# Layer 0's product with its weights from seven products of blocks

## The chip, the cores and the metric

The kernel runs on one core of one Trainium2 chip. The metric is the device time of one execution in microseconds (us). Engines: PE (TensorE, matmuls; PEld its weight loads), DVE (VectorE), ACT (ScalarE), POOL (GpSimd) and SP (SyncE, which issues DMAs). Everything is 32-bit floating point; a matmul in this type leaves two records in the trace, so 16 matmuls are 32 records.

## The reference

There are 64 sequences of 32 rows of 512 values. Two layers follow each other, each with a residual connection. The change is in layer 0:

```
u = _L0_cond_ref(x, length, ...)      # masked convolution along the 512 positions, one kernel per row h, by FFT
h = relu(layernorm(u @ gw1.T + gb1) * ln_gamma + ln_beta)      # 32 values per token
gates = h @ gw2.T + gb2                                        # 8 experts
top_v, top_i = top_k(gates, 2);  top_g = softmax(top_v)
w = onehot(top_i) * top_g * (counts <= capacity)
main = u @ weight.T                                            # 2048 x 512 by 512 x 512  <- the product that is changed
lora = sum over experts of (u @ lora_A[e] * w[e]) @ lora_B[e] / 16
x = x + main + lora
```

Layer 1 (gated projections with adapters, then a mixture of 16 experts and a shared one) takes the rest of the time and is not touched.

## The kernel before

Tokens are the 64 x 32 pairs of sequence and row h, 2048 in all, in four blocks (`tb` 0 to 3) of `TB` = 512, which are eight rows h of 64 sequences. Features lie on the 128 partitions in `NC` = 4 chunks. `xT[tb]` is the residual stream of a block, 128 x 4 x 512, and `yT` the convolution's result of a block in the same form. `w0` holds the layer's weights as 128 x 4 chunks x 512 outputs, and behind them the adapters' second matrix.

PE, DVE and ACT run in the order in which the program is written (`tc.manual_schedule`); what waits at the head of an engine's queue holds all that is behind it. DMA issues of SP and POOL have their own queues. One block goes as follows:

- `convolved` (L511, L518), eight times: four matmuls by Toeplitz blocks `g`, which SP loads from `kpad` in memory, two rows h at a time; the result `y` is in one of two PSUM banks of `ps_mm`, and DVE masks it into `yT` (L518). In between stand two DVE steps of the next block's convolution kernels (`steps`, `kgen`). After the second row, `counted` (L584) adds the block before's choices up in the bank `cn`; it needs `oh`.
- `by_tokens` (L528, L535, L536), four times: `gt`, tokens by features; DVE takes the 32 gate features (`hg`), ACT the adapters' (`tmp`).
- In block 2, `gathered_down` (L466) copies adapter rows into `wr` on ACT.
- `main` (L589) for output chunk 0; `later.products` (L329, `kp`); on DVE `normed` (L543 to L559), whose square root is on ACT (L549, with a table load); `later.to_memory` (L334, L336), after which ACT writes `kpad` (L338); in block 2 `combine` (L212 to L215), in block 0 `table_rows` (L411 to L417) and zeros (`none`, L633) that POOL writes to `yd` (L636).
- `main` for chunk 1 in two halves, with `turned` (L564, `hgT`) between them; `gated` (L572, `gates`); `main` for chunk 2; on DVE `chosen` (L578, L165 to L171), twelve small dependent operations that end in `oh`; `added` (L598) for chunks 0 and 1; `main` for chunk 3; `added` for chunks 2 and 3.

The four results of `main` lie in banks of the pool `ps_acc`, which has four, one of them held by `cn` once counting has begun. Block 3 has no later block; its third and fourth part stand with the end of the layer (`weighed`, `across`, `raised`). Layer 1 already forms one of its own products from seven products of blocks (a function `seven` and the helper `TH` = 256 there); layer 0 does not.

Of the kernel before, what the change touches and what calls it, by code (L numbers as in the profile page):

```python
# [9 lines left out]
F32 = mybir.dt.float32  # L10
I32 = mybir.dt.int32
AF = mybir.ActivationFunctionType
ALU = mybir.AluOpType
# [4 lines left out]
P = 128  # L18
B, H, L = 64, 32, 512
NS = 64  # L20
TB, NTB = 512, 4
HB = TB // B
NC = L // P
# [80 lines left out]
def kernel(ctx: ExitStack, tc: tile.TileContext, a: dict, out: bass.AP):  # L104
    nc = tc.nc
    mm, tt, ts = nc.tensor.matmul, nc.vector.tensor_tensor, nc.vector.tensor_scalar
# [8 lines left out]
    ps_acc = ctx.enter_context(tc.tile_pool(name="ps_acc", bufs=4, space=PSUM))  # L115

    def bank(pool, name):
        return pool.tile([P, TB], F32, tag="bank", name=name)
# [11 lines left out]
    wl0 = first.enter_context(tc.tile_pool(name="wl0", bufs=1))  # L130
# [44 lines left out]
    xT = [xall[:, :, tb * HB : (tb + 1) * HB, :] for tb in range(NTB)]  # L175
    xT = [x.rearrange("p c h b -> p c (h b)") for x in xT]
    nc.sync.dma_start(xT[0], a["xT"][0])
    w0 = wl0.tile([P, NC + 1, L], F32, name="w0")
# [47 lines left out]
    def small(n=H):  # L226
        part = next(r for r in room if r[1] >= n)
        part[1] -= n
        return part[0][:, part[1] : part[1] + n]
# [8 lines left out]
    def run(*streams):  # L238

        while streams:  # L240
            streams = [x for x in streams if next(x, run) is not run]
# [34 lines left out]
    start = small(1)  # L276
# [70 lines left out]
    rden, t0, t1 = small(), small(), small()  # L347
# [50 lines left out]

    for _ in range(5):
        mm(bank(ps_mm, "unread"), ident, xT[0][:, 0, :], start=True, stop=True)  # L400
    second.products()
    second.to_memory()

# [46 lines left out]
    def columns(g, j):  # L450

        lo = j // NJ * RK
        src = got[g][0][:, :, lo : lo + RK, NC + j % NJ].rearrange("p (h s b) r -> p s h b r", h=2, s=2)
        for half in range(2):
            at = half * (TW + L // 2)
            to = wn[:, j, :, at : at + TW].rearrange("p s (b r) -> p s b r", r=RK)
            nc.vector.tensor_copy(to, src[:, :, half])
# [15 lines left out]
    with tc.tile_pool(name="l0", bufs=1) as l0, tc.tile_pool(name="l0b", bufs=2) as l0b:  # L473
# [45 lines left out]
            if tb in (1, 2):  # L519
                coming[0].rows(1)  # L520

        def by_tokens(tb, yT):

            for i in range(4):
                n = tb * 4 + i
                gt = bank(ps_td, f"gt_{n}")
                for c in range(NC):
                    mm(  # L528
                        gt[:, 0 : G0 + P],
                        yT[:, c, i * P : (i + 1) * P],  # L530
                        ag[:, c, :],
                        start=(c == 0),
                        stop=(c == NC - 1),
                    )
                tt(hg[:, n, :], gt[:, 0:G0], row0[:, 0:G0], ALU.add)  # L535
                nc.scalar.copy(tmp[tb][:, i, :], gt[:, G0 : G0 + P])  # L536

        def normed(tb):

            ns = slice(tb * 4, tb * 4 + 4)  # L540
            h, m, v, r, w = hg[:, ns, :], mu[:, ns], var[:, ns], rstd[:, ns], nw[:, ns]
            sq = l0b.tile([P, 4, G0], F32, tag="sq", name=f"sq_{tb}", bufs=1)
            red(m, h, AX.X, ALU.add)  # L543
            ts(m, m, 1.0 / G0, None, ALU.mult)
            tt(h, h, over(m, G0), ALU.subtract)
            tt(sq, h, h, ALU.mult)
            red(v, sq, AX.X, ALU.add)
            ts(v, v, 1.0 / G0, 1e-5, ALU.mult, ALU.add)
            nc.scalar.activation(r, v, AF.Sqrt)  # L549
            nc.vector.reciprocal(r, r)  # L550

            tt(w, r, r, ALU.mult)
            tt(w, w, v, ALU.mult)
            ts(w, w, -0.5, 1.5, ALU.mult, ALU.add)
            tt(r, r, w, ALU.mult)
            tt(h, h, over(r, G0), ALU.mult)
            tt(h, h, rows(row0[:, G0 : 2 * G0], 4), ALU.mult)
            tt(h, h, rows(row0[:, 2 * G0 : 3 * G0], 4), ALU.add)
            ts(h, h, 0.0, None, ALU.max)  # L559
# [21 lines left out]
        def counted(tb):  # L581

            for n in range(tb * 4, tb * 4 + 4):
                mm(cn[:, 0 : 2 * E0], ones, oh[:, :, n, :], start=(n == 0), stop=(n == NT - 1))  # L584

        def main(yT, ps, o, cs=range(NC)):

            for c in cs:
                mm(  # L589
                    ps,  # L590
                    w0[:, c, o * P : (o + 1) * P],
                    yT[:, c, :],
                    start=(c == 0),
                    stop=(c == NC - 1),
                )

        def added(tb, o, ps):
            tt(xT[tb][:, o, :], xT[tb][:, o, :], ps, ALU.add)  # L598

        toeplitz, coming = [], []  # L600
        for tb in range(NTB):
            if tb == 1:
                coming.append(Adapters(0))
                got = [coming[0].all()]
            yT = l0b.tile([P, NC, TB], F32, tag="yT", name=f"yT_{tb}")

            later = Kernels((tb + 1) * HB) if tb + 1 < NTB else None
            steps = later.steps() if later is not None else iter(())
            for hl in range(HB):
                convolved(tb, hl, yT)  # L610
                next(steps, None)
                next(steps, None)
                if hl == 1 and tb > 0:
                    counted(tb - 1)
                if tb == NTB - 1:
                    for j in range(hl, NF, HB):
                        columns(0, j)
            by_tokens(tb, yT)
            run(steps)
            if tb == 2:  # L620
                wr = gathered_down(0)
            ps = [bank(ps_acc, f"main_{tb}_{o}") for o in range(2)]
            main(yT, ps[0], 0)
            if later is not None:
                later.products()
            normed(tb)
            if later is not None:
                later.to_memory()
            if tb >= 2:
                combine(tb - 2)  # L630
            if tb == 0:
                table_rows()
                nc.vector.memset(none, 0.0)  # L633
                for t in range(NTU, NTE):
                    rest = yd[t * P : (t + 1) * P, :].rearrange("p (c l) -> p c l", l=P)
                    nc.gpsimd.dma_start(rest, rows(none, NC))  # L636
            main(yT, ps[1], 1, range(2))
            hT = turned(tb)
            main(yT, ps[1], 1, range(2, NC))
            gp = gated(tb, hT)  # L640
            if tb == NTB - 1:

                nc.scalar.activation(l0.tile([P, 1], F32, name="one_exp"), col(C_SGN), AF.Exp)
            ps.append(bank(ps_acc, f"main_{tb}_2"))
            main(yT, ps[2], 2)
            chosen(tb, gp)
            if tb < NTB - 1:
                added(tb, 0, ps[0])
                added(tb, 1, ps[1])
                ps.append(bank(ps_acc, f"main_{tb}_3"))  # L650
                main(yT, ps[3], 3)
                added(tb, 2, ps[2])
                added(tb, 3, ps[3])


        tt(sg[:, 1, :], best[:, 1, :], best[:, 0, :], ALU.subtract)
# [289 lines left out]
    for g in range(NG):  # L946
# [3 lines left out]
        for j in range(NF):  # L950
# [10 lines left out]
            ps = bank(ps_mm, f"gu_{g}_{j}")  # L961
# [12 lines left out]
            more = bank(ps_mm, f"gum_{g}_{j}")  # L974
# [56 lines left out]
    acc, pools, wall, places = [], [], [], []  # L1031
    routing = ExitStack()
    wide = ExitStack()

    TH = TB // 2

    def quarters(tb):

        return [xT[tb][:, k : k + 2, lo : lo + TH] for k in (0, 2) for lo in (0, TH)]

# [12 lines left out]
    def seven(tb, j, banks, si, at, done):  # L1053

        b11, b12, b21, b22 = quarters(tb)
        t1, t2, t3, t4 = diffs[tb]
        gate, up = (x.rearrange("p (k t) -> p k t", k=2) for x in (si, at))

        def products(k, *parts):
            ps = bank(banks[k % len(banks)], f"sgu_{tb}_{j}_{k}").rearrange("p (k t) -> p k t", k=2)  # L1060
            for i, (w, x) in enumerate(parts):
                w = sw[j][:, w * BW :] if w < 4 else ssw[j - 1][:, (w - 4) * BW :]
                for c in range(2):
                    mm(ps[:, i, :], w[:, c * P : (c + 1) * P], x[:, c, :], start=(c == 0), stop=(c == 1))  # L1064
            return ps

        ps = products(0, (0, b11), (6, b22))
        nc.scalar.copy(gate, ps)
        ps = products(1, (1, b21), (4, t2))
        tt(up[:, 0], gate[:, 0], ps[:, 1], ALU.add)  # L1070
        tt(gate[:, 0], gate[:, 0], ps[:, 0], ALU.add)
        tt(gate[:, 1], gate[:, 1], up[:, 0], ALU.add)
        done("gate", j)
        ps = products(2, (3, t4), (5, t3))
        tt(up[:, 1], up[:, 0], ps[:, 1], ALU.add)
        tt(up[:, 0], up[:, 1], ps[:, 0], ALU.add)
        ps = products(3, (2, t1))
        tt(gate[:, 1], gate[:, 1], ps[:, 0], ALU.add)
        tt(up[:, 1], up[:, 1], ps[:, 0], ALU.add)
# [471 lines left out]
```

## Time and profile before

| | us |
|---|---|
| median of 3 runs | 1020.14 (1019.03 to 1020.51) |
| profiled execution, its own time | 1020.05 |
| its span, first to last instruction | 1018.3 |
| PE busy in the span | 987.4 (97%) |
| DVE busy | 648.3 (64%) |
| ACT busy | 212.0 (21%) |
| block 0 of layer 0, first y to the next block's first y | 23.89 to 54.08 |
| block 1 | 54.08 to 85.07 |
| block 2 | 85.07 to 116.05 (the third's last product ends at 116.92) |
| granted TensorE clock, mean | 1.000 |

The page's row of an instruction group names line, engine, operation, output and input, count, then busy time, mean duration in ns, and the idle time of the engine just before with the work that ended it. Durations of matmuls overlap, so what one costs in a stream is read from start to start. A timeline's row has the start and the length in us, then the same names, and in brackets the idle time before it and who ended it.

### The profile page before, as it was taken

The numbers are of one execution on the slowest core, as the hardware profiler recorded it, in microseconds if no ns is written. First come the engines' busy times: TensorE is split into PE (matmuls) and PEld (weight loads), VectorE is DVE, ScalarE is ACT, GpSimd is POOL, SyncE is SP. The second block draws the span as 40 slices with busy tenths as digits, with TensorE's granted clock in tenths as the row PEclk, the third lists the DMA queues.
The fourth block names the chain that finished last, engine by engine and source line by source line (L and its number), as shares of the span: only waits on it lengthen the run. The fifth ranks groups of instructions, "written<-read, shape, count | busy, mean of one in ns | idle before, by whom it ended". The sixth has DMA issues, their size and how long they took to land. (4 is left out here: it accounts for less than half of the span.)

```text
span 1018.3 us, 16926 instructions
## 1 busy us (share of the span) xinstructions
PE 987.4 (97%) x6256; PEld 792.2 (78%) x6256; DVE 648.3 (64%) x1974; ACT 212.0 (21%) x439; POOL 170.1 (17%) x189
## 2 busy tenths in 40 slices
PE   3999999999999999999999999999999999999998
PEld 1777656888988889988889888897767677776665
DVE  6656567887666776766676767765765353333775
ACT  2322111121221311213212122121201222221100
POOL 2131001210301202102012021000000333331730
PEclk9999999999999999999999999999999999999999
DMA  6566408685665646746567557540940455555652
GB/s 187 191 224 232 136 21 301 236 294 174 224 199 192 238 164 213 248 161 214 186 198 257 175 189 238 172 141 17 409 188 1 133 167 166 166 165 199 200 176 95
DMA packets 64210, 190.62 MB, mean 187 GB/s; under 512 B 8512, under 2 KB 11616, under 8 KB 63488
## 3 DMA queue, kind: packets, MB, share of 16 engines
q1 hardware_dynamic: 49360, 138.30, 39.2%
q0 software_dynamic: 14176, 51.16, 16.2%
q8 instruction: 52, 0.85, 0.3%
q14 instruction: 30, 0.25, 0.1%
q10 hardware_dynamic: 592, 0.07, 0.1%
HBM read 158.35 MB, written 31.15 MB: 186 GB/s over the span
## 5 line engine op out<-in xcount | busy, mean ns | idle before, releaser
L885 PE MATMUL zp<-wn,at 128*128 128x288 f32 x704 | 185.4, 406 | 0.4 <-DVE at L984 0.4
L819 PE MATMUL gu<-t,w 128*128 128x128 f32 x1056 | 150.1, 278 | 0.9 <-DVE gus L966 0.9
L885 PEld LDWEIGHTS zp<-wn,at 128*128 128x128 f32 x704 | 127.1, 190 | 28.6 <-DVE at L984 0.6
L819 PEld LDWEIGHTS gu<-t,w 128*128 128x128 f32 x1056 | 135.4, 192 | 14.8 <-DVE gus L966 6.4
L444 POOL DMA_INDIRECT wa<-in_la,row_a x64 | 61.2, 956 | 299.9 <-issue 183.4
L982 ACT ACTIVATE si<-gus 128x256 f32<-128x256 f32 x88 | 36.7, 417 | 350.5 <-DVE gus L980 350.5
L819 PE MATMUL gum<-xall,w 128*128 128x128 f32 x704 | 93.0, 275 | 0.0
L819 PEld LDWEIGHTS gum<-xall,w 128*128 128x128 f32 x704 | 85.7, 192 | 0.0
L1327 PE MATMUL egu<-wall,zx 128*128 x336 | 80.6, 383 | 0.4 <-issue 0.4
L966 DVE TENSOR_TENSOR gus<-gu,los 128x512 f32<-128x512 f32 x88 | 60.6, 688 | 28.7 <-PE gu L819 26.2
L960 DVE TENSOR_TENSOR los<-los 128x512 f32<-128x512 f32 (+1 forms) x72 | 46.6, 647 | 49.9 <-ACT los L839 48.3
L1327 PEld LDWEIGHTS egu<-wall,zx 128*128 128x128 f32 x336 | 60.5, 189 | 20.0 <-ACT zx L1318 13.0
L984 DVE TENSOR_TENSOR at<-si,gus 128x256 f32<-128x256 f32 x88 | 37.4, 425 | 48.2 <-ACT si L982 48.2
L1308 POOL DMA_INDIRECT zr<-zd,tok x42 | 39.7, 946 | 159.4 <-PE zrp L1316 86.3
L839 ACT COPY los<-lo 128x512 f32<-128x512 f32 (+1 forms) x96 | 46.6, 560 | 60.1 <-PE lo L836 60.1
L1099 PE MATMUL op<-sat,sw 128*128 128x512 f32 x128 | 58.0, 595 | 0.6 <-DVE sat L1124 0.3
L589 PE MATMUL main<-yT,w 128*128 128x512 f32 x128 | 58.4, 599 | 0.0
L836 PEld LDWEIGHTS lo<-rs,wb 64*128 64x128 f32 x704 | 42.6, 187 | 16.0 <-issue 10.6
L836 PE MATMUL lo<-rs,wb 64*128 64x128 f32 x704 | 48.0, 279 | 6.1 <-DVE gus L980 5.5
L819 PE MATMUL gum<-t,w 128*128 128x128 f32 x352 | 53.7, 275 | 0.0
L819 PE MATMUL gu<-xall,w 128*128 128x128 f32 x352 | 53.7, 275 | 0.0
L1347 DVE COPY eys<-ey 128x512 f32<-128x512 f32 x42 | 29.1, 692 | 29.7 <-PE ey L1345 29.7
(316 smaller groups left out, 1452.0 us busy)
## 6 DMA issues: line engine op xcount, KB each, us to landing
w<-sums_d SPq DMA_DIRECT2D x77, 512.0 KB, 4.8
w<-in_cw SPq DMA_DIRECT2D x77, 384.0 KB, 3.4
wall<-in_xw SPq DMA_DIRECT2D x16, 768.0 KB, 15.1
yd<-eys SPq DMA_DIRECT2D x42, 256.0 KB, 2.8
g<-kpad SPq DMA_DIRECT2D x15, 512.0 KB, 5.5
w<-in_cw SPq DMA_DIRECT2D x11, 512.0 KB, 4.7
sums_d<-w SPq DMA_DIRECT2D x9, 512.0 KB, 3.6
xall<-in_xT SPq DMA_DIRECT2D x4, 1024.0 KB, 8.6
```

The lines of the kernel that those rows point to most:

```text
L444: nc.gpsimd.indirect_dma_start(to, None, src, at)
L589: mm(ps, w0[:, c, o * P : (o + 1) * P], yT[:, c, :], start=(c == 0), stop=(c == NC - 1),)
L819: mm(to, block(n, i)[:, c * P : (c + 1) * P], x[:, c], start=(c == 0), stop=(c == 1))
L836: mm(banks[which][:, at : at + P], wb[mine, lo : lo + P], r[mine, half, :], start=True, stop=True)
L839: nc.scalar.copy(to[:, first - j : first - j + n, 2 * which : 2 * which + 2], src)
L885: mm(self.zp[half][s][:, 0 : DW - TW], at[:, 1 - half, :], wn[:, j, s, lo : lo + DW - TW], start=(j == 0), stop=(j == NF - 1),)
L960: tt(lo[:, :, i], lo[:, :, i], lo[:, :, less], ALU.subtract)
L966: tt(flat, ps, adapters[:, j % 4].rearrange("p k t -> p (k t)"), ALU.add)
L984: tt(at, si, flat[:, TG:], ALU.mult)
L1099: mm(op[o], sw[j][:, i : i + P], at, start=(j == 0), stop=(j == NS1 - 1))
L1308: nc.gpsimd.indirect_dma_start(zr, None, zd[:, :], bass.IndirectOffsetOnAxis(ap=tok[:, t : t + 1], axis=0))
L1327: mm(ps[:, 0:256], x[:, c, :], wflat()[:, bass.ds(start + c * 256, 256)], start=(c == 0), stop=(c == NC - 1))
```

## The change

For blocks 0 to 2 the product of a 512 x 512 weight with a 512 x 512 block of `yT` is cut into halves of the features, of the outputs and of the tokens. Seven products of 256 x 256 x 256 blocks take the place of eight; each is four matmuls of 128 x 128 weights with 256 columns. Their operands are sums and differences: four sums of the weights (`w_sum`) are made once on DVE before the first convolution, and four differences of `yT` in every block, after each of the four tiles of `by_tokens` (the fourth is written over the part b12 of `yT`). The seven products use five banks per block: the product w12 b21 is added by PE to the bank of w11 b11 after ACT has copied that to `u`, and s4 b22 to the bank of s1 t1 after DVE has read it. DVE adds up `u` and the banks into `xT` in nine operations instead of four. `seven` is a generator; each `next(parts)` in the loop issues its next stretch, so the parts stand between the norm, `turned`, `gated` and `chosen`. After `gated` no product is left in these blocks, and the last two additions follow `chosen`. Block 3 is as before.

```diff
+    TH = TB // 2
+    w_sum = wl0.tile([P, 4, 2, TH], F32, name="w_sum")
+    w11, w12, w21, w22 = (w0[:, c : c + 2, o : o + TH] for o in (0, TH) for c in (0, 2))
+    s1, s2, s3, s4_ = (w_sum[:, i] for i in range(4))
+    tt(s1, w21, w22, ALU.add)
+    tt(s2, s1, w11, ALU.subtract)
+    tt(s3, w11, w21, ALU.subtract)
+    tt(s4_, w12, s2, ALU.subtract)
     second.products()
     second.to_memory()
...
-        def by_tokens(tb, yT):
+        def by_tokens(tb, yT, between=iter(())):
...
                 nc.scalar.copy(tmp[tb][:, i, :], gt[:, G0 : G0 + P])
+                next(between, None)
...
+        def seven(tb, yT, ps):
+            b11, b12, b21, b22 = (yT[:, c : c + 2, t : t + TH] for c in (0, 2) for t in (0, TH))
+            x11, x12, x21, x22 = (xT[tb][:, o : o + 2, t : t + TH] for o in (0, 2) for t in (0, TH))
+            diff = l0.tile([P, 3, 2, TH], F32, name=f"diff_{tb}", tag="diff")
+            t1, t2, t4 = (diff[:, i] for i in range(3))
+            t3 = b12
+            yield tt(t1, b12, b11, ALU.subtract)
+            yield tt(t2, b22, t1, ALU.subtract)
+            yield tt(t4, b21, t2, ALU.subtract)
+            yield tt(t3, b22, b12, ALU.subtract)
+            u = l0.tile([P, 2, TH], F32, name=f"u_{tb}", tag="u")
+
+            def onto(to, w, x, more=False):
+                for o in range(2):
+                    for c in range(2):
+                        nc.tensor.matmul(
+                            to[:, o],
+                            w[:, c, o * P : (o + 1) * P],
+                            x[:, c],
+                            start=(not more and o == 0 and c == 0),
+                            stop=(c == 1),
+                            skip_group_check=True,
+                        )
+
+            m1, m6 = ps(), ps()
+            onto(m1, w11, b11)
+            nc.scalar.copy(u, m1)
+            onto(m6, s2, t2)
+            yield
+            tt(u, u, m6, ALU.add)
+            tt(x12, x12, u, ALU.add)
+            onto(m1, w12, b21, True)
+            m7 = ps()
+            onto(m7, s3, t3)
+            yield
+            tt(x11, x11, m1, ALU.add)
+            tt(u, u, m7, ALU.add)
+            m5 = ps()
+            onto(m5, s1, t1)
+            tt(x21, x21, u, ALU.add)
+            tt(x22, x22, u, ALU.add)
+            yield
+            m4 = ps()
+            onto(m4, w22, t4)
+            tt(x22, x22, m5, ALU.add)
+            onto(m5, s4_, b22, True)
+            yield
+            tt(x21, x21, m4, ALU.add)
+            tt(x12, x12, m5, ALU.add)
...
-            by_tokens(tb, yT)
+            last = tb == NTB - 1
+            parts = iter(()) if last else seven(tb, yT, one)
+            by_tokens(tb, yT, parts)
             run(steps)
             if tb == 2:
                 wr = gathered_down(0)
-            ps = [bank(ps_acc, f"main_{tb}_{o}") for o in range(2)]
-            main(yT, ps[0], 0)
+            if last:
+                ps = [bank(ps_acc, f"main_{tb}_{o}") for o in range(2)]
+                main(yT, ps[0], 0)
+            next(parts, None)
             if later is not None:
                 later.products()
             normed(tb)
...
-            main(yT, ps[1], 1, range(2))
+            next(parts, None)
+            if last:
+                main(yT, ps[1], 1, range(2))
+            next(parts, None)
             hT = turned(tb)
-            main(yT, ps[1], 1, range(2, NC))
+            if last:
+                main(yT, ps[1], 1, range(2, NC))
+            next(parts, None)
             gp = gated(tb, hT)
...
-            main(yT, ps[2], 2)
+                main(yT, ps[2], 2)
             chosen(tb, gp)
-            if tb < NTB - 1:
-                added(tb, 0, ps[0])
-                added(tb, 1, ps[1])
-                ps.append(bank(ps_acc, f"main_{tb}_3"))
-                main(yT, ps[3], 3)
-                added(tb, 2, ps[2])
-                added(tb, 3, ps[3])
+            next(parts, None)
```

More of the change, by code (lines that the diff above doesn't have):

```diff
@@ L617, with one @@
                         columns(0, j)
-            by_tokens(tb, yT)
+            banks = []
+            def one():
+                banks.append(bank(ps_acc, f"main_{tb}_{len(banks)}"))
+                return banks[-1].rearrange("p (o t) -> p o t", o=2)
+            last = tb == NTB - 1
+            parts = iter(()) if last else seven(tb, yT, one)
+            by_tokens(tb, yT, parts)
             run(steps)
@@ L636 @@
                     nc.gpsimd.dma_start(rest, rows(none, NC))
-            main(yT, ps[1], 1, range(2))
+            next(parts, None)
+            if last:
+                main(yT, ps[1], 1, range(2))
+            next(parts, None)
             hT = turned(tb)
-            main(yT, ps[1], 1, range(2, NC))
+            if last:
+                main(yT, ps[1], 1, range(2, NC))
+            next(parts, None)
             gp = gated(tb, hT)
-            if tb == NTB - 1:
+            if last:
                 nc.scalar.activation(l0.tile([P, 1], F32, name="one_exp"), col(C_SGN), AF.Exp)
-            ps.append(bank(ps_acc, f"main_{tb}_2"))
-            main(yT, ps[2], 2)
+                ps.append(bank(ps_acc, f"main_{tb}_2"))
+                main(yT, ps[2], 2)
             chosen(tb, gp)
-            if tb < NTB - 1:
-                added(tb, 0, ps[0])
-                added(tb, 1, ps[1])
-                ps.append(bank(ps_acc, f"main_{tb}_3"))
-                main(yT, ps[3], 3)
-                added(tb, 2, ps[2])
-                added(tb, 3, ps[3])
+            next(parts, None)
         tt(sg[:, 1, :], best[:, 1, :], best[:, 0, :], ALU.subtract)
@@ L1033 @@
     wide = ExitStack()
-    TH = TB // 2
     def quarters(tb):
```

## The prediction

> **What bounds the kernel now.** I read the page first, then the busy time of each engine block by block, then the timelines of TensorE, VectorE and ScalarE in one block.
>
> ```profile
> PE 987.4 (97%) x6256; PEld 792.2 (78%) x6256; DVE 648.3 (64%) x1974; ACT 212.0 (21%) x439; POOL 170.1 (17%) x189
> L589 PE MATMUL main<-yT,w 128*128 128x512 f32 x128 | 58.4, 599 | 0.0
> ```
>
> TensorE is the bound over the whole span, and the product that the change touches is 58.4 us of it with no idle time before it. Three of its four blocks change. By stage:
>
> ```profile
> 23.89:54.08 30.19, 30.19 (x159) 21.37 (x157) 18.79 (x70) 8.52 (x13) 3.72 (x5) 1.00 0.65 219
> 54.08:85.07 30.99, 30.99 (x165) 22.09 (x164) 18.27 (x70) 7.24 (x12) 7.80 (x8) 1.00 0.57 194
> 85.07:116.05 30.98, 30.28 (x163) 21.64 (x162) 19.62 (x69) 8.13 (x15) 3.53 (x4) 1.00 0.58 193
> ```
>
> Columns: stretch, length, then busy PE, PEld, DVE, ACT, POOL, clock, DMA. PE is full in the first two blocks and lacks 0.70 us in the third; DVE is busy 18 to 20 us of 31, so about 12 us free per block. How those free microseconds lie is what decides. Block 1 on PE (start, length, work):
>
> ```profile
> 68.95 3.60 PE L589 MATMUL main<-yT,w 128*128 128x512 f32 x8
> 72.48 0.64 PE L329 MATMUL kp<-kgen 128*16 128x32 f32 x16
> 73.05 1.98 PE L589 MATMUL main<-yT,w 128*128 128x512 f32 x4
> 74.87 0.60 PE L564 MATMUL hgT<-cst,hg 128*32 128x128 f32 x4
> 75.31 1.88 PE L589 MATMUL main<-yT,w 128*128 128x512 f32 x4
> 77.12 1.05 PE L572 MATMUL gates<-gw,hT 32*128 32x8 f32 x8
> 78.10 7.13 PE L589 MATMUL main<-yT,w 128*128 128x512 f32 x16
> 85.07 2.51 PE L511 MATMUL y<-xall,g 128*128 128x256 f32 x16
> ```
>
> From start to start the product takes 3.53 + 1.82 + 1.81 + 6.97 = 14.13 us for 16 matmuls (32 records). The last 6.97 us come after gates, and that is the cover for what DVE does then:
>
> ```profile
> 78.21 0.19 DVE L578 TENSOR_TENSOR gates_sb<-gates,row 128x32 f32<-128x32 f32 x1 [4.09 <-PE gates L572]
> 80.79 1.88 DVE L598 TENSOR_TENSOR xall<-xall,main 128x512 f32<-128x512 f32 x3
> 85.27 0.69 DVE L598 TENSOR_TENSOR xall<-xall,main 128x512 f32<-128x512 f32 x1 [2.61 <-PE main L589]
> 86.42 0.43 DVE L518 TENSOR_TENSOR yT<-y,mlen 128x256 f32<-128x256 f32 x1 [0.46 <-PE y L511]
> ```
>
> The choice of experts runs from 78.21 to 80.79, and DVE then has slack until the next block's first y. On ACT in block 2 stands one long piece ahead of the square root that the norm waits for:
>
> ```profile
> 100.53 2.29 ACT L466 COPY wr<-wa 128x256 f32<-128x256 f32 x4
> 102.83 1.28 ACT L549 ACT_TABLE_LOAD   x1
> 104.12 0.20 ACT L549 ACTIVATE rstd<-var 128x4 f32<-128x4 f32 x1
> ```
>
> **The change, part by part.** I count from the start of a block's gt (L528), at 33.56, 64.55 and 95.54.
>
> TensorE's work. 28 matmuls of 256 columns (56 records) take the place of 16 of 512 (32 records). The nearest rows of such records in a stream:
>
> ```profile
> 599.93 2.11 PE L885 MATMUL zp<-wn,at 128*128 128x288 f32 x8
> 601.87 0.61 PE L819 MATMUL gu<-t,w 128*128 128x128 f32 x4
> ```
>
> 8 records of 288 columns in 1.94 us are 0.84 ns a column, 1.73 us for 8 of 256. This product itself runs at 3.53 us for 8 of 512, 0.86 ns a column, so 1.77 us; bounds 1.73 and 1.84. I take 1.77 for one of the seven products, 12.39 us for all: 1.74 us less per block. [...] But the trace has 32 records with their loads in 14.13 us and 8 of 288 columns in 1.94 us, so loads are hidden, and at 256 columns 190 ns still fit under 216. I go by the rows.
>
> Sums of weights, once: four DVE adds of 512 elements, at 0.59 us (three adds in 1.88) to 0.72 (0.69 and a dependence). They stand between 20.71 and 23.4 us, where DVE idles 3.28 us until kp comes from PE at 23.99; the weights have landed by then (issued at 2.4 us, 13.6 us to landing). Cost nothing. Without that cover it would be 2.7 us once.
>
> Before the norm: four adds per block. Three fit in the 0.90 us gaps between the gt tiles; the fourth is before the norm, +0.6 us. ACT gets a copy of the first product, which PE ends at 4.40 + 1.77 = 6.17: copy 6.4 to 6.95 (0.57, as the tw copies), and only then the table load of 1.28 us and the square root, at 8.26 instead of 6.60. The norm ends 1.65 us later. hgT no longer suffers: it now stands behind five products (13.8 us), and block 2's 0.70 us wait goes. But what is queued behind the norm on DVE does: the kernel rows for memory (ready at 11.2, was 9.5), and then the adds that free PE's banks.
>
> Those waits, by block. u += m6 ends at 11.8 at the earliest, x11 += m1 at 13.1, u += m7 at 13.7, then x21, x22, and x22 += m5 at 15.8. PE comes to m5 at 12.05, to m4 at 14.26, to the second part of m5 at 16.03.
> - Block 1: all are just in time. gates ends at 18.78 instead of 20.52: -1.74.
> - Block 0: the table of rows and the zeros (43.06 to 44.37) stand ahead of u += m6, so x22 += m5 ends 1.4 later, at 17.15, and PE waits 1.24 us: 20.02 instead of 20.52, -0.50.
> - Block 2: the wr copies put the square root at 9.34 instead of 8.58, and combine's four adds (1.8 us) also stand ahead of u += m6. It ends at 14.66; its bank is the one that m5 needs, and PE waits 2.73 us. Next block at 21.51 instead of 21.38: +0.13.
>
> After gates. It is now PE's last work in a block. DVE needs 0.11 + 2.6 us for the choice, then two adds (1.2), then the first y's mask (0.43): done 4.25 us after the first y begins, was 1.78 (86.85 against 85.07). PE has only y, y, counts: 1.21 + 1.21 + 0.87. counts waits for the choice (0.42), the third y for the first mask since y has two banks (0.66), later y's in blocks 0 and 1 for DVE's long steps of 128x384 (0.34): +1.42, +1.42, and +1.08 before block 3, where the steps are shorter.
>
> Queues. The SP loads of g follow the rows for memory and come 1.65 us later in blocks 0 and 1, 0.6 in 2. In block 0 the first lands at about 44.74 + 1.65 + 6.0 = 52.4, needed at 53.6; in 1 and 2 the margins are 2.2 and 1.5 us. POOL's zeros (L636) start 1.6 us later, nobody waits. The memsets that release the gathers shift by about a microsecond; their rows are read 30 us later.
>
> Sum: -0.50 - 1.74 + 0.13 + 1.42 + 1.42 + 1.08 = +1.8 us. PE is full after that, so it stays to the end. The profiled execution has 1020.05 us (span 1018.3 and 1.75 around it), so 1021.85; the median of the runs is 0.09 above it: 1021.9.
>
> [...] The trace shows clock 1.00 through block 2 with its 0.70 us wait and nothing longer in this stage. [...]
>
> **The rivals.**
> - Faster: the seven products keep their 1.74 us per block and the waits mostly vanish, because DVE's adds overlap more than my walk allows or m5 finds a bank. With half of the 7.9 us of waits gone, -2.1 us: 1018.0; with all, -5.9: 1014.2. For it: DVE has 12 us free per block. Against: after gates the order is fixed, and 12 dependent operations at 0.22 us cannot shrink. It decides below about 5.8 us of waits.
> - Late g: landing of g ranges from 3.8 to 10.5 us in the trace. If block 0's first takes 9 instead of 6, the first y waits 1.8 us: 1023.7; with 10.5 it waits 3.3: 1025.2. It decides once a landing exceeds 7.2 us.
> - Loads not hidden: if each record at 256 columns takes 0.26 us (0.216 and a fifth of a load), a product takes 2.1 us, and 21 of them add 6.9 us less what the waits swallow, about 1026. The 288-column row speaks against it.
> - That the program isn't what it says: the order of the built program has 28 matmuls of 256 columns in each of the three blocks, so this is out.
>
> **How the numbers follow.** About 0.2% (2 us) is what a measurement of this kernel can tell from no change, so the line is at 1018.1 and 1022.2. The walk as above has 0.65, with its own range 1020.4 to 1023.8 (product at 1.73 to 1.84, signal from DVE to PE 0.05 to 0.2 us): a little more than half of it within the line. Faster has 0.17, late g 0.11, loads 0.07. Same: 0.37 + 0.03 = 0.40; slower 0.28 + 0.15 = 0.43; faster 0.17. Range 1018.0 to 1025.0.
>
> **What would show it.** Right: records of L626 at about 0.22 us from start to start; DVE's wait before gates_sb shorter than 4.09; PE waits for DVE before counts and the third y of blocks 1 to 3, before m5 in block 2 and before m5's second part in block 0; none in block 1's product. Wrong: PE full after gates (then faster), a wait of y for g, or records well over 0.23 us.

## The result and the profile after

The changed kernel takes 1023.02 us, the median of 15 runs (1020.89 to 1026.42), where the kernel before takes 1019.78 us, the median of 15 (1018.61 to 1022.9), on the same chip. The ratio is 1.0034, 95% interval 1.0022 to 1.0047: slower by 3.2 us. The profiled execution is the slowest of the 15, 1026.42 us with a span of 1024.6; before's span was 1018.3.

From the page of the changed kernel, busy time of PE and DVE:

```profile
PE 987.4 (96%) x6328; PEld 809.1 (79%) x6328; DVE 666.9 (65%) x2005; ACT 213.9 (21%) x442; POOL 169.9 (17%) x189
```

PE has 72 records more (3 x 24) and the same busy time as before, but two stretches at half clock, below, are in this sum. DVE has 18.6 us more. Block 1 on the timeline of PE is the part that went as meant:

```profile
75.88 1.89 PE L626 MATMUL main<-yT,w_sum 128*128 128x256 f32 x8
77.61 1.89 PE L626 MATMUL main<-diff,w_sum 128*128 128x256 f32 x8
79.33 0.60 PE L575 MATMUL hgT<-cst,hg 128*32 128x128 f32 x4
...
83.32 1.05 PE L583 MATMUL gates<-gw,hT 32*128 32x8 f32 x8
84.31 2.62 PE L521 MATMUL y<-xall,g 128*128 128x256 f32 x16
87.13 1.06 PE L595 MATMUL counts<-oh,cst 128*128 128x16 f32 x8 [0.20 <-DVE oh L169]
88.66 7.60 PE L521 MATMUL y<-xall,g 128*128 128x256 f32 x48 [0.46 <-DVE wb L453]
```

From 75.88 to 77.61 eight records take 1.73 us, 0.216 us each. No row of the product has a bracket. Two of the three rows after gates have one: PE waits there for the last operation of the choice, and for a bank of `y` that DVE has not read yet (the releaser printed, `wb`, is a small memset that stands right behind the mask on DVE). On DVE in the same block:

```profile
84.41 0.19 DVE L589 TENSOR_TENSOR gates_sb<-gates,row 128x32 f32<-128x32 f32 x1 [3.07 <-PE gates L583]
...
88.19 0.41 DVE L528 TENSOR_TENSOR yT<-y,mlen 128x256 f32<-128x256 f32 x1
```

The first mask ends at 88.60, 4.29 us after PE began the first `y` (84.31). Block 2 on PE, and then lines of the list of PE's waits (total, times, longest):

```profile
110.59 3.60 PE L626 MATMUL main<-diff,w_sum 128*128 128x256 f32 x8 [2.26 <-DVE u L640]
114.03 0.60 PE L575 MATMUL hgT<-cst,hg 128*32 128x128 f32 x4
```

```profile
PE lo L909 <- DVE gus L1053: 6.2, 5, 1.4
PE main L626 <- DVE u L640: 2.3, 1, 2.3
PE lo L909 <- DVE gus L1039: 1.2, 1, 1.2
...
PE main L626 <- DVE xall L655: 0.9, 1, 0.9
PE counts L595 <- DVE oh L169: 0.7, 3, 0.3
```

The product m5 waits 2.26 us for `u` += m6, which reads the bank that m5 is to take, and then takes 3.44 us from its start to the next instruction's instead of 1.8: it ran at half clock. The busy time by stretch says so in its clock column (before: 1.00 in the same stretch):

```profile
86.00:118.00 32.00, 29.08 (x171) 25.50 (x170) 23.60 (x71) 8.63 (x16) 3.49 (x4) 0.95 0.60 202
```

ACT and DVE in block 2 show why `u` is late:

```profile
101.08 2.29 ACT L476 COPY wr<-wa 128x256 f32<-128x256 f32 x4
103.27 0.59 ACT L637 COPY u<-main 128x512 f32<-128x512 f32 x1
103.88 1.28 ACT L560 ACT_TABLE_LOAD   x1
105.17 0.20 ACT L560 ACTIVATE rstd<-var 128x4 f32<-128x4 f32 x1
...
109.42 0.42 DVE L215 TENSOR_TENSOR w<-w 128x256 f32<-128x256 f32 x1
109.76 0.68 DVE L640 TENSOR_TENSOR u<-u,main 128x512 f32<-128x512 f32 x1
```

The square root stands behind four copies, the copy of m1 and the table load; DVE's norm, `combine` (its last row is L215) and only then `u` += m6 (L640) stand behind the square root.

Behind block 2 this execution lost as much again. The first `gt` of block 3 starts 3.24 us later than before's (130.62 against 127.38) and the span ends 6.3 us later. In layer 1 PE and DVE show:

```profile
217.13 0.48 PE L909 MATMUL lo<-rs,wb 64*128 64x128 f32 x2 [1.24 <-DVE gus L1039]
218.98 2.22 PE L909 MATMUL lo<-rs,wb 64*128 64x128 f32 x22 [1.37 <-DVE gus L1053]
```

```profile
216.01 0.47 DVE L467 COPY wn<-wa 128x64 f32<-128x64 f32 x3 [1.90 <-DMA wa<-in_la,row_a]
```

A gather of adapter rows landed 1.90 us after DVE wanted it (0.54 us in before), PE waited twice, and a second stretch at half clock follows (22 records take 2.22 us; 1.57 in before). Layer 1's code is the same in both kernels.

### The profile page after: what moved, and what is told of

The parts are those of the page before. It is cut to its first block, busy times and chain, and to the rows that moved or that the text cites. A ratio compares the mean times of both kernels' runs of the same rounds, so it can differ in the third digit from the quotient of the medians.

```text
span 1024.6 us, 17108 instructions
## 1 busy us (share of the span) xinstructions
PE 987.4 (96%) x6328; PEld 809.1 (79%) x6328; DVE 666.9 (65%) x2005; ACT 213.9 (21%) x442; POOL 169.9 (17%) x189
## 5 line engine op out<-in xcount | busy, mean ns | idle before, releaser
L892 PEld LDWEIGHTS gu<-xall,w 128*128 128x128 f32 x352 | 46.8, 194 | 0.0
```

What stands on the lines that cost most here:

```text
L892: mm(to, block(n, i)[:, c * P : (c + 1) * P], x[:, c], start=(c == 0), stop=(c == 1))
```

## Theories

- A: PE's saving is there, and the loss is order: waits before m5 in blocks 0 and 2, and after gates in all three, because DVE and ACT come to the needed step late.
- B: the nine additions are simply too much DVE work for the block, whatever the order.
- C: the gather in layer 1 is late because of the change (its position in DVE's instruction stream, or what is issued before it), and this is the larger part of the loss.
- D: the half clock after the 2.26 us wait is what makes +1.5 us into +3.2.

The expectations have letters of their own; those in the headings below are the ones of this list.

## The experiments

Each is told with its ratio to the kernel before, which ran beside it.

**The wait filled (D).** Two matmuls of 512 columns whose result nobody reads, before m5 of block 2.

```
             m5 = ps()
+            for _ in range(2 if tb == 2 else 0):
+                mm(bank(ps_mm, "unread"), ident, w0[:, 0, :], start=True, stop=True)
             onto(m5, s1, t1)
```

> The changed kernel with two matmuls of 128x512 into an unread bank put on PE just before m5 of block 2, where PE waits 2.3 us for u += m6. They do no work of the result. Theory A (the clock dropped because that wait left PE idle): the wait's length stays, since DVE sets it, but m5 runs at 0.22 us a record instead of 0.44 and the clock of 86 to 118 us is 1.00: 1.7 us less than the changed kernel in executions that had the drop, about +1.5 us against before. Theory B (the drop is a chance event of the run and not of the wait): clock drops there as often as before, no gain, about +3.2 us against before.

Measured: 1023.71 us, ratio 1.0028 (1.0015 to 1.0041), not to be told from the changed kernel's 1.0034. Of its 10 executions 5 have a mean granted clock of 0.998 or less, of the changed kernel's 15 there are 9. (A stretch of 3.4 us at half clock makes 0.998 of a mean over 1020 us.) PE's timeline of block 2:

```profile
107.74 1.88 PE L650 MATMUL unread<-w,cst 128*128 128x512 f32 x4
110.17 1.97 PE L626 MATMUL main<-diff,w_sum 128*128 128x256 f32 x8 [0.55 <-DVE u L640]
```

The wait is 0.55 us and the product runs at full clock. m5 starts at the same place, since it is DVE that decides. But the median has not moved by 1.7, so the half clock cannot be a toll that every execution pays at this wait. Theory D does not stand as it was put; the last experiment says more.

**DVE's and ACT's order (A against B).** In block 2 the copies to `wr` are issued after the norm; `combine` of block 2 and the row tables and zeros of block 0 go behind the last addition that frees a bank.

```
-            if tb == 2:
-                wr = gathered_down(0)
             ...
             normed(tb)
+            if tb == 2:
+                wr = gathered_down(0)
             ...
-            if tb >= 2:
+            if last:
                 combine(tb - 2)
-            if tb == 0:
+
+            def rest_of_block():
+                if tb == 2:
+                    combine(tb - 2)
+                if tb != 0:
+                    return
                 table_rows()
             ...
             next(parts, None)
+            rest_of_block()
             gp = gated(tb, hT)
```

> The changed kernel with the other DVE and ACT work taken out from ahead of the adds: the wr copies of block 2 after the norm's square root, combine(0) of block 2 and the table of rows and zeros of block 0 after x22 += m5, in DVE's gap before gates. Theory A (what stands ahead of the adds on DVE and ACT makes the waits in blocks 0 and 2): the wait before m5 in block 2 (2.3 us), the slow m5 behind it (1.7 us) and the wait in block 0 (0.9 us) go, the waits after gates stay: 4.9 us less than the changed kernel, -1.7 us against before (about 1018.3). Rival (the wait is due to the late product m6 or to banks): the wait before m5 stays, no gain.

Measured: 1019.84 us, ratio 1.0001 (0.9989 to 1.0013), where about 1018.3 was expected. PE has no wait left in the product in any block; in block 2, m5 and what follows it:

```profile
106.77 1.89 PE L626 MATMUL main<-diff,w_sum 128*128 128x256 f32 x8
108.50 0.60 PE L575 MATMUL hgT<-cst,hg 128*32 128x128 f32 x4
```

The first `gt` of blocks 0 to 3 start at 33.52, 64.13, 94.69 and 125.10: 91.58 us for three blocks, where before took 93.82 and the changed kernel 96.88 in its profile. The waits after gates are as they were (counts 0.29, 0.20, 0.20; `y` 0.40, 0.47, 0.47). That layer 0 gained 2.2 us and the median is level is the clock: six executions with a mean clock of 1.0 have a median of 1018.3, as expected, and the other eight, at 0.998 or less, one of 1021.9.

**Cover after gates (A against B).** `turned` moves ahead of m5 and `gated` ahead of m4, so that two products (3.5 us) follow gates.

```
-            next(parts, None)
             hT = turned(tb)
+            next(parts, None)
             ...
-            next(parts, None)
             gp = gated(tb, hT)
+            next(parts, None)
```

> The changed kernel with hgT moved ahead of m5 and gates ahead of m4, so that two products (3.5 us of PE) stand between gates and the next block's first y. Theory A (the choice of experts lost its cover): the waits before counts and the third y, about 1.2 us a block, go in all three blocks: 3.5 us less than the changed kernel, about level with before; the wait of block 2 before m5 and the clock drop behind it stay. Rival (DVE is short as a whole, so its work only moves): the waits come back before m4 or m5's second part, and the gain is under 1 us.

Measured: 1019.97 us, ratio 0.9996 (0.9988 to 1.0004). Three blocks take 90.95 us. The waits of counts are gone; of `y`, two small ones are left, for the loads of `g` (0.17 and 0.32 us). The 1.82 us before m5 in block 2 are left too, this time with the clock at full. Layer 0 gained 2.9 us against before; in 11 of the 13 executions the mean clock is 0.998 or less, so this gain too is hardly seen in the median.

**Eight additions less (B).** All but one of the nine additions per block are taken out.

```
-            tt(u, u, m6, ALU.add)
             tt(x12, x12, u, ALU.add)
             ...
-            tt(x11, x11, m1, ALU.add)
-            tt(u, u, m7, ALU.add)
             ...
-            tt(x21, x21, u, ALU.add)
-            tt(x22, x22, u, ALU.add)
             ...
-            tt(x22, x22, m5, ALU.add)
             ...
-            tt(x21, x21, m4, ALU.add)
-            tt(x12, x12, m5, ALU.add)
```

> The changed kernel with eight of the nine additions of each block left out (the banks of m1, m6, m7, m5, m4 are then not read by DVE and layer 0's product does not reach the residual stream). It measures TensorE's side alone. Theory A (the seven products save 1.74 us a block on PE): no wait before m5 or m5's second part, no clock drop, only the wait of counts for the choice (0.3 us a block): -5.2 - 0.7 + 0.9 = -5.0 us against before (about 1015). Rival (256-column products cost more than half of 512-column ones): less than 3 us below before.

Measured: 1017.6 us, ratio 0.9976 (0.9967 to 0.9985), 89.34 us for three blocks. By its time, 2.8 us below before, this would be the rival's case, and about 1015 was expected. The trace says otherwise: layer 0 gained 4.5 us, and the records of the product are 0.216 us apart; in 9 of the 19 executions the mean clock is 0.998 or less. Less DVE work does help, in this order of PE's instructions: from 96.88, or 95.31 in an execution without the clock drop, to 89.34. The waits of counts are still there.

**Both reorderings (A).** The edits of the second and third experiment together, with all nine additions.

> Both reorderings together: nothing but the norm ahead of the adds in blocks 0 and 2, and hgT and gates ahead of the last two products. Theory A (the change's whole loss in layer 0 is waits made by the order on DVE and ACT): the three blocks keep nearly all of the saving on PE, block 3's first gt starts at about 121.5 us in the profile (127.4 before, 130.6 in the changed kernel), and the time is 4 to 6 us below before, less what layer 1 adds by its own waits. Rival (DVE has too little free time in a block, 12 us against some 9 us of added work): the waits come back at other places, and block 3's gt stays above 124.

Measured: 1015.48 us, ratio 0.9953 (0.9939 to 0.9966): faster than both kernels. PE in block 2:

```profile
103.99 0.60 PE L575 MATMUL hgT<-cst,hg 128*32 128x128 f32 x4
104.43 1.89 PE L626 MATMUL main<-diff,w_sum 128*128 128x256 f32 x8
106.25 1.05 PE L583 MATMUL gates<-gw,hT 32*128 32x8 f32 x8
...
110.79 2.52 PE L521 MATMUL y<-xall,g 128*128 128x256 f32 x16
113.14 1.02 PE L595 MATMUL counts<-oh,cst 128*128 128x16 f32 x8
```

No bracket is left. Each of the three blocks takes 29.34 us (33.23, 62.57, 91.91, 121.25): 88.02 in all, 5.8 less than before, with all of DVE's additions done. Theory B falls: DVE has room, if the order gives PE what it needs first. 30.99 - 29.34 = 1.65 us is PE's saving in blocks 0 and 1, 1.74 in the prediction; block 2 took 31.84 before, with a wait of 0.70 us for `hgT` that is gone too.

**The place in the instruction stream (C).** The kernel before with 31 tiny memsets on DVE in layer 0 (10, 11 and 10 in blocks 0 to 2), as many instructions as the change adds there.

> The kernel before with 31 one-column memsets on DVE in front of the choice of experts in blocks 0 to 2, where DVE is idle; so DVE's instruction stream has the length that it has in the changed kernel. In the changed kernel's trace DVE waits 1.90 us in layer 1 (near 216 us) for a gather of wa, before 0.54. Theory C (the longer stream moves a fetch of instructions onto that gather): DVE's wait there becomes about 1.9 us and PE's before lo two waits of 1.2 and 1.4; 1 to 2 us above before. Theory D (the length of the stream is not it): the wait stays near 0.5, level with before within 0.5 us.

Measured: 1019.79 us, ratio 0.9996 (0.9987 to 1.0005). It is level, and the wait for `wa` at that place is 0.33 us. In this one profile the length of DVE's stream did not make the gather late. What PE, ACT and the DMA queues issue otherwise was not varied.

**Gathered rows used one step later (C).** In the changed kernel, what layer 1 does with gathered rows starts at step 7 instead of 6; the same edit was also made to the kernel with both reorderings.

```
-            if g + 1 < NG and 6 <= j:
-                if j == 6:
+            if g + 1 < NG and 7 <= j:
+                if j == 7:
             ...
-                for i in ((0, 1), (2, 3), (4, 5), (6, 7), (8,))[j - 6]:
+                for i in ((0, 1, 2), (3, 4), (5, 6), (7, 8))[j - 7]:
```

> The changed kernel with layer 1's use of the gathered adapter rows (the wr copies and the columns of wn for the next group) one step later in each group, so that the gather has 5 us more to land. Layer 0 is as in the changed kernel. Theory E (a good part of the +3.2 us is in layer 1: the gather that lands late holds DVE, PE waits 1.2 us more before lo, and the two waits together at times drop the clock): DVE's wait for wa goes, and the time is 1.2 to 2.5 us below the changed kernel. Rival (all of the loss is in layer 0): level with the changed kernel.

> Both reorderings in layer 0 and the later use of the gathered rows in layer 1. If theories A and E hold, the parts add up: about 6 us below before from layer 0 and up to 1 us from layer 1, 1013 to 1015 us; if either is wrong, it stands where the other alone stands.

Measured: 1023.59 us, ratio 1.0043 (1.003 to 1.0056), and 1015.76 us, ratio 0.9962 (0.9949 to 0.9975). Neither gained. The wait for the gather went and PE's waits before `lo` fell to 1.2 us, but PE then waited for copies on ACT (seven times before `gu`, 7.3 us in all), probably because the work squeezed into fewer steps was in ACT's way. A miss: it moved the wait.

**Gathers issued earlier (C), and the same programs again.** The same rows are used at the same step as before, but three gathers a step are issued at first instead of two; once in the changed kernel, once in the one with both reorderings.

```
-                coming[-1].rows(2 if j < 6 else 1)
+                coming[-1].rows(3 if j < 4 else 2)
```

> The changed kernel with layer 1's gathers of rows issued three a step for the first four steps and then two, instead of two for six and then one; layer 0 is as in the changed kernel. If the late gather in layer 1 (VectorE's wait of 1.90 us for wa, with TensorE's 1.24 and 1.37 us behind it, and the second half-clock stretch) is a part of the loss beyond layer 0, the wait for wa falls under 0.6 us and the time is 1 to 2.5 us below the changed kernel: 1020.5 to 1022. If layer 1's gather is only beside the point (the loss is layer 0's 1.35 us and its clock drop), the time stays at 1023 within 0.5 us whether the wait goes or not.

> Both reorderings of layer 0 and the earlier issue of layer 1's gathers. If the gather costs anything after the reordering, 1013 to 1014.5; if not, it stays at 1015.5 as with the reorderings alone. Above 1016.5 the earlier gathers themselves get in the way of something.

> The changed kernel again, one profile. If the late gather in layer 1 belongs to the kernel, VectorE's wait for wa at about 216 us is 1.3 to 1.9 us again; if it belongs to the one execution, it is near 0.5 us as in the kernel before. The wait of 2.26 us before m5 in block 2 should recur; whether the next product runs at half clock again is open.

> The kernel before again, one profile: the wait for wa near 0.5 us if the late gather belongs to the changed kernel, 1.3 us or more if it comes and goes by execution. No half-clock stretch in layer 0.

Measured: 1018.1 us, ratio 0.9976 (0.9964 to 0.9988), more than was expected; and 1010.35 us, ratio 0.99 (0.9885 to 0.9915), the best of all. PE's waits before `lo` in all of layer 1, in the changed kernel run again and with earlier gathers:

```profile
PE lo L909 <- DVE gus L1053: 6.3, 5, 1.4
```

```profile
PE lo L909 <- DVE gus L1053: 2.5, 5, 1.0
```

3.8 of the 4.0 us between the two spans (1020.3 and 1016.3) are there. But this is no part of what the change lost: the kernel before has the same wait, 5.5 us in its profile. The edit was not tried on it.

The repeats do not settle theory C. The changed kernel again took 1022.1 us, and its wait for `wa` in that place was 0.53 us, not 1.90: the same program has it both ways. But three other profiles with the changed order on DVE and ACT have the gather late at the same place (the wait filled, cover after gates, eight additions less):

```profile
214.03 0.47 DVE L467 COPY wn<-wa 128x64 f32<-128x64 f32 x3 [1.86 <-DMA wa<-in_la,row_a]
209.08 0.47 DVE L467 COPY wn<-wa 128x64 f32<-128x64 f32 x3 [1.29 <-DMA wa<-in_la,row_a]
207.57 0.46 DVE L467 COPY wn<-wa 128x64 f32<-128x64 f32 x3 [1.79 <-DMA wa<-in_la,row_a]
```

That is four of five profiles. The three with before's layer 0 have 0.54, 0.58 and 0.33 us there, and the two with DVE's and ACT's order mended and the gathers as they were 0.59 and 0.58. So the late gather may well come with the changed order; ten profiles do not prove it, and in later groups before's own waits reach 1.67 us. The larger part of the loss it is not: the repeat, without it, still took 1022.1 us. In the repeat of the changed kernel the 2.26 us before m5 came back, and the clock stayed at full:

```profile
109.98 1.97 PE L626 MATMUL main<-diff,w_sum 128*128 128x256 f32 x8 [2.26 <-DVE u L640]
111.79 0.60 PE L575 MATMUL hgT<-cst,hg 128*32 128x128 f32 x4
```

The kernel before again took 1022.85 us, with a stretch at half clock of its own, in a later group of layer 1:

```profile
483.13 0.48 PE L836 MATMUL lo<-rs,wb 64*128 64x128 f32 x2 [0.50 <-DVE gus L966]
484.99 2.74 PE L836 MATMUL lo<-rs,wb 64*128 64x128 f32 x22 [1.37 <-DVE gus L980]
```

From the first `gt` of block 3 to the end of the span the two executions of the changed kernel took 894.0 and 891.9 us, those of before 890.9 and 893.9: the same program differs by 2.1 and by 3.0 us there from one execution to the next.

## Why the prediction came out

1021.9 was predicted and 1023.02 measured, inside the range of 1018.0 to 1025.0. The walk through layer 0 was right in its mechanism, and makes 1.5 of the 3.2 us. For the rest the prediction had no term, only the width of its range; that the median fell inside is in part luck. Step by step, with the changed kernel's second execution, which no clock drop disturbs in layer 0, beside the first:

| us | before | predicted | first profile | again |
|---|---|---|---|---|
| block 0, first `gt` to first `y` after it | 20.52 | 20.02 | 19.96 | 19.96 |
| block 1 | 20.52 | 18.78 | 18.78 | 18.79 |
| block 2 | 21.38 | 21.51 | 22.91 | 21.35 |
| after gates, `y` to next `gt`, block 0 | 10.47 | 11.89 | 11.83 | 11.82 |
| block 1 | 10.47 | 11.89 | 11.78 | 11.78 |
| block 2 | 10.46 | 11.54 | 11.62 | 11.61 |
| sum | 93.82 | 95.63 | 96.88 | 95.31 |

- PE's saving: 1.77 us a product was taken, 1.73 is the row. Weight loads stay hidden: in block 1 of the changed kernel the product's loads take 190 ns each on PEld, as they did in before, and the matmul records of 256 columns still start 0.216 us apart. The block gained 1.74 us. No run shows the 0.26 us a record of the rival in which loads are not hidden.
- The norm behind the copy of m1 on ACT, and the waits it makes before m5: 2.73 predicted and 2.26 measured in block 2, 1.24 and 0.92 in block 0, none in block 1, as predicted. Counted from the block's first `gt`, DVE's addition that frees the bank ended at 14.35 in block 2 and 17.00 in block 0, where the walk had 14.66 and 17.15. The rest of the difference is that a bracket is counted from the modelled end of the matmul before it, the walk from start to start.
- After gates: +1.42, +1.42, +1.08 predicted, +1.35, +1.31, +1.15 measured in the second execution. The mask ends 4.29 us after the first `y` starts, 4.25 in the walk. This is the largest part of the loss, and the brackets alone undersell it (0.20 and 0.46 us in block 1). From start to start the two first `y`, counts and the other six `y` take 2.82, 1.53 and 7.43 us in block 1; with no wait, in block 2 of before, 2.35, 0.86 and 7.25:

```profile
116.92 2.51 PE L511 MATMUL y<-xall,g 128*128 128x256 f32 x16
119.27 1.02 PE L584 MATMUL counts<-oh,cst 128*128 128x16 f32 x8
120.13 7.41 PE L511 MATMUL y<-xall,g 128*128 128x256 f32 x48
127.38 4.57 PE L528 MATMUL gt<-ag,yT 128*128 128x160 f32 x32
```

That is +0.47, +0.67 and +0.18, where 0.42, 0.66 and 0.34 were predicted. The sign that DVE's wait before `gates_sb` falls below 4.09 came true in block 1, from which it was read (3.07). In blocks 0 and 2 that wait rose, from 2.86 to 3.07 and from 1.26 to 4.19.

- `g` was not late: no `y` waits for it in the changed kernel.
- Sum in layer 0: +1.81 predicted, +1.49 measured where the clock stayed up.

The term that is missing is the clock. The prediction's sum has none: in before the clock is 1.00 through block 2, where PE's wait is 0.70 us, and the walk puts a wait of 2.73 us there. In the first profile the half clock behind that wait cost 1.57 us (34.53 for block 2 against 32.96 again). The half-clock stretches in mid span last 3.413 us in the traces, one of them twice that. Counted in such lengths from PE's first full clock they start at 26.0 and 58.0 in the first profile, at 136.0 in before's second, at 56.0 in two of the experiments (cover after gates, eight additions less) and at 174.0 in the kernel with both reorderings. So they lie on a grid of windows of that length, whose place to the kernel's work differs from run to run. The slow m5 starts with its window (110.59 and 110.50; from 110.50 to 113.91 the clock column has 0.50), and the window ahead, at 1.00, held 2.17 us of idle PE and 1.2 us of work: it was not idle throughout.

So the error was to leave the clock at 1.00 for a wait of 2.73 us, when before's block 2 shows it only beside one of 0.70. How much of the wait falls into one window differs from profile to profile. In the three other profiles with this wait uncovered (the changed kernel again, rows used later, gathers earlier) a border of the grid cuts it: at most 1.86, 1.73 and 1.67 us of idle PE lie in one window, and the clock stayed up. If it falls where the wait lies wholly inside a window, that is (3.413 - 2.26) / 3.413, about one time in three, and 0.5 us on average: an estimate worked out from these numbers and not set by an experiment. Idle time alone does not decide it: ahead of the other five stretches a window holds 2.18, 1.87, 2.00, 2.36 and, with both reorderings, only 1.47 us of it.

Among the changed kernel's 15 timed executions, 6 have a mean granted clock of 0.999 or 1.0 and a median of 1022.26; 59 of the 76 executions of before that ran beside the experiments do, with a median of 1020.07. That is +2.2 us with the clock up. Layer 0 accounts for 1.5 of it; the other 0.7 was not traced to a place. The other 9 of 15 have 0.998 or less and a median of 1025.4, and only 17 of 76 of before. So about 1 of the 3.2 us is that the clock falls more often.

Where it falls more often points to layer 1. Five of the six stretches follow PE's waits before `lo` there, and three of these five stand right behind the late gather (the first profile, cover after gates, eight additions less). With the gathered rows used later or the gathers issued earlier, 5 of 25 executions have 0.998 or less (2 of 5 and 3 of 11 with the changed layer 0, 0 of 5 and 0 of 4 with both reorderings); the same two versions of layer 0 with the gathers as they were have 12 of 21 (9 of 15 and 3 of 6). Both edits also shorten the waits before `lo` that before has too, so it stays open whether the changed layer 0 makes the gather late, or only moves where on the grid those waits fall. Nor is it known why one gather lands 1.3 us later in one execution than in another.

The rival that ended faster (the waits vanish) was not what the changed kernel does, but it is what both reorderings make of it: -5.9 us was written for all waits gone (the prediction's own sum, 1.81 less 7.89, is -6.1), and layer 0 then gave -5.80.

## What to carry to other kernels

Fewer matmul columns pay only if the engines that read the results are asked in the order in which TensorE runs out of banks and cover: list the operation that frees the next bank and what stands ahead of it on its in-order engine, then leave matmuls behind the small dependent chain whose result the next stage needs. Here the same seven products cost 3.2 us in one order and gave 4.4 us (ratio 0.9953) in another. Before a late transfer or a slow stretch is charged to a change, or cleared of it, look at it in several executions of both programs: the first pair of profiles made the late gather look like the change's, one repeat made it look like chance, and ten profiles leave it open. And look at the granted clock of every timed run: it hid gains of 2 to 3 us in the median here.

## What was not expected of the hardware

A wait of 2.26 us was followed by 3.413 us at half clock in one execution, in which 2.17 us of it lay in one window beside 1.2 us of work, and not in three others, where the border of a window cut the wait. Pairs of waits of 0.50 and 1.37 us and of 1.24 and 1.37 us, with half a microsecond of matmuls in between, were also followed by it; a pair of 1.21 and 1.37 us (the wait filled) was not, and there the border lay between the two. And three gathers a step instead of two, with the same rows used at the same step, took 3.8 us off waits in layer 1 that the versions without an edit there all carried.
